# Four-layer kernel: layer 2's rows, projections and later norms prepared in another order

## The chip, the cores and the metric

The kernel runs on one core of a Trainium2 chip. The metric is the device time of one execution in microseconds. A profiled execution gives, besides its time, the work of each engine: TensorE (PE, with its weight loads shown apart as PEld), VectorE (DVE), ScalarE (ACT), GpSimd (POOL) and SyncE (SP), and the clock that TensorE was granted, as a share of full speed.

## The reference

Two sequences of 1024 tokens with 128 features pass four layers. Every layer has the same frame:

```python
xn = _layernorm(x, axis=-1)
s = attn(xn)                 # another kind of attention in each layer
g = _silu(ffn(xn))
x = x + s * g
```

The change is in layer 2. Its branch s is linear attention: a layer norm of xn (eps 1e-5, with weights), a projection to q, k, v, a gate, and running sums:

```python
x_norm = (x - mu) / jnp.sqrt(var + 1e-05) * ln_g + ln_b
q, k, v = jnp.split(x_norm @ w_qkv + b_qkv, 3, axis=-1)
gate_sig = jax.nn.sigmoid(x @ w_gate + b_gate)
gate_norm = gate_sig / (jnp.mean(gate_sig, axis=-1, keepdims=True) + 1e-05)
q, k = elu(q * gate_norm) + 1.0, elu(k * gate_norm) + 1.0
# causal: out = q . cumsum(k v) / (q . cumsum(k) + 1e-05), then w_proj
```

Its branch ffn is a small transformer block: causal softmax attention (16 heads of 8 features, 4 groups that share keys and values), then a mixture of 8 experts of which each token takes 2:

```python
def rms_norm(x, w): return x / jnp.sqrt(jnp.mean(x * x, -1, keepdims=True) + 1e-06) * w
# rope on even and odd features: [xe * cos - xo * sin, xe * sin + xo * cos]
h = x + attention(rms_norm(x, norm1_w), Wq, Wk, Wv, Wo)   # Q, K, V all from rope(x)
h = h + moe(rms_norm(h, norm2_w), router_w, router_b, W1, b1, W2, b2, W3, b3)
```

The input x of both branches is xn, which already is a layer norm. Its mean over the features is 0, and its mean square is var / (var + 1e-5), from the moments of the x before it.

## The kernel before

The 2048 tokens are 16 tiles of 128 tokens (rows), in 4 groups of 4 tiles, 512 tokens each; groups 0 and 1 are the first sequence, 2 and 3 the second. A matrix product needs its input with features as rows, so tiles are transposed on PE (four 128x128 transposes into one PSUM bank, `to_feature_major`, line 293), and copied to SBUF by ACT or DVE in turn (`copy`, lines 282 and 284). All products go through one helper (line 287), so PE's rows are told apart by their tiles.

**End of layer 1.** For each group the experts' rows are summed (`fetch`, line 398), passed through SiLU (989), multiplied (990) and added to x (991), in the order of groups 0, 2, 1, 3.

**Layer 2, preparation.** `normalise` (line 320) takes the moments of a group's x (statistics and their aggregation, lines 310 and 311; the root on ACT between a DVE addition and a DVE reciprocal, 299 to 301), makes xn on DVE (325), and transposes it into xT. Then `Attention.prepare` (1338), for each sequence and group: the sum of squares of xn on ACT (333), a root, xw = xn times the row's factor times the norm's weights on DVE (1352), the rotation as four products, a difference and a sum on POOL (1360 to 1365), the transposes of the rotated rows xr into xrT; and after both groups of a sequence the products with the weights: kT (pk), four qT (pq), and va (pv). kT and qT are kept as a rounded part and a remainder: `parts` casts on ACT (1335) and then runs one DVE operation (1336). PSUM has 8 buffers here.

**Softmax attention** (`softmax_attention`, 1510) first makes its constants on DVE (1518 to 1524): rounded identity, ones, two masks, and four cleared tiles mp. Then come four pre-steps (-4 to -1) and 72 steps, one for each pair of a query tile and a key tile not after it. To know each query row's largest score ahead of its exponentials, the scores are computed twice: once as pm, with queries as rows, for the maxima (`maxima`, 1397; DVE's reduction, 1424; the negated maxima split in mp, 1436 and 1437; turned on PE as pmt and copied to mT, 1444), and once as psc, with keys as rows (`weights`, 1448), on which ACT runs the exponential (1468), and whose results PE multiplies with va (pat, `values`). `close` (1480) divides, projects and adds xn: h. `take` (1534) decides how many pieces of maxima go into a step, from what is left and when it is due. The pieces pm, pmt and those of `close` share three PSUM buffers (sm2, tag pm); psc has two of two banks, pat has one.

PE's instructions stand in the order in which this code is written (`manual_schedule`, line 1012). The orders of the other engines are made by a scheduler of the framework, in the whole program.

**After it**: the norm of h, the router, and `Dispatch`, which makes the lists of rows for each expert (up to dfrom, line 1176), and the first part of linear attention. `linear_attention` (1222) is a generator, run forward a group at a time at the start, in the middle and at the end of the expert blocks. For each group it takes moments of xn, makes xl (1242), transposes it to xlT, multiplies with wq (128x384) and xT with the gate's weights, adds the biases (qg), and goes on to the gate (sig, gsum), qk (1263 to 1267), kv (1280) and the running sums. The expert blocks (1055 to 1078) load 256 rows each, and DVE, ACT and PE take part in all.

Of the kernel before, what the change touches and what calls it, by code (L numbers as in the profile page):

```python
# [19 lines left out]
P = 128  # L20
# [252 lines left out]
class Kern:  # L273
# [46 lines left out]
    def normalise(self, pool, ps, x, xn, xT, xs=None):  # L320
        for g in range(NG):
            mv, rs = self.moments(pool, lambda j: x[:, g * G + j, :], G, 1e-5, "ln")
            for j in range(G):
                i = g * G + j
                self.nc.vector.tensor_scalar(xn[:, i, :], x[:, i, :], mv[:, j, 0:1], rs[:, j : j + 1], ALU.subtract, ALU.mult)  # L325
            if xs is not None:
                keep_rows(self, xs, xn, g)
            self.to_feature_major(ps, lambda i: xn[:, i, :], xT, g)
# [665 lines left out]
def layer2(K, x, xn, xT, w, inp):  # L994
# [3 lines left out]
    with ExitStack() as es:  # L998
# [3 lines left out]
        with ExitStack() as e1:  # L1002
            pf = e1.enter_context(tc.tile_pool(name="f2", bufs=1))
            seqs = [Attention(K, pf, xn, w, h, b) for b in range(NB)]
            with tc.tile_pool(name="sn2", bufs=8, space=PSUM) as sn, tc.tile_pool(name="p2", bufs=1) as pp:
                K.normalise(pp, sn, x, xn, xT)
                for a in seqs:
                    a.prepare(pp, sn)
# [3 lines left out]
            with tc.manual_schedule(engines={mybir.EngineType.PE}):  # L1012
                with ExitStack() as e3:
# [3 lines left out]
                    softmax_attention(K, pf, sm, sc, so, seqs)  # L1017
        with ExitStack() as e2:
# [20 lines left out]
            linear = linear_attention(K, pa, sa, xn, xT, w, s)  # L1039
# [182 lines left out]
def linear_attention(K, pa, sa, xn, xT, w, s):  # L1222
# [7 lines left out]
    wq, bq = two("wq", [P, 384]), two("bq", [P, 512])  # L1230
# [4 lines left out]
    nc.vector.tensor_scalar_mul(wq, w["wqkv"], w["g"])  # L1235
    for g in range(NG):
        first = g % (NG // NB) == 0
        kvs = nc.vector if g < NG // NB else nc.gpsimd
        xl = two("xl", four)
        mv, rs = K.moments(pa, lambda j: xn[:, g * G + j, :], G, 1e-5, "la")  # L1240
        for j in range(G):
            nc.vector.tensor_scalar(xl[:, j, :], xn[:, g * G + j, :], mv[:, j, 0:1], rs[:, j : j + 1], ALU.subtract, ALU.mult)
        pt = sa.tile(four, F32, name="pxl", tag="ps")
        for j in range(G):
            nc.tensor.transpose(pt[:, j, :], xl[:, j, :], c["ident"])
        xlT = two("xlT", four)
        K.copy(xlT, pt)
        qg = two("qg", [P, G, 512], 2)
        sig, gsum = two("sig", four), two("gsum", [P, G])
        for j in range(G):  # L1250
            i = g * G + j
            pq = sa.tile([P, 512], F32, name="pqg", tag="ps")
            K.mm(pq[:, :384], xlT[:, j, :], wq)
            K.mm(pq[:, 384:], xT[:, i * P : (i + 1) * P], w["wg"])
            nc.vector.tensor_add(qg[:, j, :], pq, bq)
# [65 lines left out]
class Attention:  # L1321
# [16 lines left out]
    def prepare(self, pp, sc):  # L1338
        K, pf, xn, w, b = self.K, self.pf, self.xn, self.w, self.b
        nc, c = K.nc, K.c  # L1340
        four = [P, G, P]
        xrT = pp.tile([P, SEQ], F32, name="xrT", bufs=2)
        rs = pp.tile([P, TPB], F32, name="ars", bufs=2)
        for g in range(TPB // G):
            tiles = range(b * TPB + g * G, b * TPB + g * G + G)
            gr = rs[:, g * G : (g + 1) * G]
            for j, i in enumerate(tiles):
                K.sumsq(pp, gr[:, j : j + 1], xn[:, i, :])
            K.rsqrt(gr, gr, 1.0 / P, 1e-6)
            xw = pp.tile(four, F32, name="xw", bufs=2)  # L1350
            for j, i in enumerate(tiles):
                nc.vector.scalar_tensor_tensor(xw[:, j, :], xn[:, i, :], gr[:, j : j + 1], w["n1"], ALU.mult, ALU.mult)
            pair = xw.rearrange("p t (f two) -> p t f two", two=2)
            xe, xo = pair[:, :, :, 0], pair[:, :, :, 1]
            at = slice(g * G, g * G + G)
            cos, sin = w["cos"][:, at, :], w["sin"][:, at, :]
            xr = pp.tile(four, F32, name="xr", bufs=2)
            t2 = pp.tile([P, G, 64], F32, name="t2", bufs=2)
            t3 = pp.tile([P, G, 64], F32, name="t3", bufs=2)
            nc.gpsimd.tensor_mul(xr[:, :, :64], xe, cos)  # L1360
            nc.gpsimd.tensor_mul(t2, xo, sin)
            nc.gpsimd.tensor_sub(xr[:, :, :64], xr[:, :, :64], t2)
            nc.gpsimd.tensor_mul(xr[:, :, 64:], xe, sin)
            nc.gpsimd.tensor_mul(t3, xo, cos)
            nc.gpsimd.tensor_add(xr[:, :, 64:], xr[:, :, 64:], t3)
            K.to_feature_major(sc, lambda i: xr[:, i % G, :], xrT, g)
        self.qT = qT = pf.tile([P, 4, SEQ], F32R, name="qT", bufs=2)
        self.kT = kT = pf.tile([P, SEQ], F32R, name="kT", bufs=2)
# [3 lines left out]
        for g in range(TPB // G):  # L1372
            cols = slice(g * 512, (g + 1) * 512)
            pk = sc.tile([P, 512], F32, name="pk", tag="ps")
            K.mm(pk, w["wk"], xrT[:, cols])
            self.parts(pp, kT[:, cols], pk, w["klow"])
            for j in range(4):
                pq = sc.tile([P, 512], F32, name="pq", tag="ps")
                K.mm(pq, w["wq"][:, j, :], xrT[:, cols])
                self.parts(pp, qT[:, j, cols], pq, w["qlow"])  # L1380
            pv = sc.tile([P, G, 32], F32, name="pv", tag="ps")
            for j in range(G):
                i = g * G + j
# [96 lines left out]
    def close(self, sb, sm):  # L1480
# [26 lines left out]
        return first, second, third  # L1507


def softmax_attention(K, pf, sm, sc, so, seqs):  # L1510

# [317 lines left out]
```

## Time and profile before

| what | us |
|---|---|
| median of three runs | 1370.8 |
| the three runs | 1370.8, 1363.27, 1372.84 |
| profiled execution, its own time | 1371.2 |
| its span (first to last instruction) | 1369.3 |
| layer 2: x of layer 1 complete | at 479.9 |
| first product of group 0's keys (pk) | at 505.26 |
| first mask of the pre-steps (pm) | at 530.46 |
| first step (psc) | at 555.26 |
| last exponential's step over | about 838.7 |
| last h | at 843.8 |
| dfrom (rows of the experts known) | at 911.3 |

The clock granted over the profiled execution was 0.887 of full speed. Times "at" count from the start of the span. A row of the timeline shows the start, the duration, the engine, the line, the operation, and out<-in tiles with their shapes; several instructions of one kind in a run are one row with a count (x4), whose duration is that of all. In square brackets stands the idle time before it and what ended it.

### The profile page before, as it was taken

To read this page: it belongs to the slowest core of one execution; us is meant where nothing else is said; L and a number is where in the kernel's file an instruction comes from. 1 tells how busy PE (TensorE), PEld (TensorE's weight loads), DVE (VectorE), ACT (ScalarE), POOL (GpSimd) and SP (SyncE) were. 2 spreads that over 40 slices of the span, in tenths; PEclk is the share of its full clock that TensorE was granted. 3 is DMA by queue.
4 is the path that set the end of the run, shared out by engine and by line. 5 is a ranking of instruction groups with operands and counts; after the bars stand their busy time and mean duration, and the time that the engine had idled before them with its cause. 6 is when DMAs were issued, how large, how long until landed. Compare 5 with 4: busy or idle time off the path is not lost. (4 is left out here: it accounts for less than half of the span.)

```text
span 1369.3 us, 19321 instructions
## 1 busy us (share of the span) xinstructions
PE 1134.2 (83%) x6861; PEld 793.5 (58%) x6861; DVE 885.1 (65%) x2216; ACT 634.7 (46%) x1072; POOL 425.2 (31%) x420
## 2 busy tenths in 40 slices
PE   5599866888898748999999998679989918799985
PEld 2277455787798425544444433458778815577664
DVE  6536445875665686577787753988657469566456
ACT  7665926215413232344455576233452316355761
POOL 0352160027455150000000000034766521467743
PEclk9899885899999757699999998769999967799997
DMA  2000003014344200000000000024344530233411
GB/s 89 0 1 1 0 15 122 1 59 157 105 136 134 62 0 1 1 1 1 1 1 1 1 1 24 8 89 117 111 131 126 155 104 24 70 85 96 78 54 47
DMA packets 49040, 75.72 MB, mean 55 GB/s; under 512 B 7335, under 2 KB 36402, under 8 KB 48688
## 3 DMA queue, kind: packets, MB, share of 16 engines
q1 hardware_dynamic: 39632, 54.30, 12.7%
q0 software_dynamic: 8448, 14.98, 5.0%
q10 hardware_dynamic: 864, 5.21, 1.1%
q8 instruction: 54, 0.88, 0.3%
q14 instruction: 42, 0.34, 0.1%
HBM read 63.95 MB, written 12.85 MB: 56 GB/s over the span
## 5 line engine op out<-in xcount | busy, mean ns | idle before, releaser
L1424 DVE TENSOR_REDUCE mx<-pm 128x1 f32<-128x512 f32 (+3 forms) x304 | 182.1, 656 | 65.6 <-PE pm L287 62.6
L1468 ACT ACTIVATE pr<-psc 128x1024 f32<-128x1024 f32 x144 | 139.6, 1021 | 103.9 <-PE psc L287 68.2
L1188 POOL DMA_INDIRECT xb<-xs,dfrom x132 | 131.7, 998 | 123.2 <-PE pxb L797 31.5
L1198 POOL DMA_INDIRECT ys<-yb,dto x132 | 137.0, 1038 | 95.3 <-DVE yb L1076 44.4
L1163 POOL TENSOR_TENSOR dhh<-dhh,w_c 128x1280 fp32r<-128x1280 f32 (+2 forms) x3 | 8.8, 2927 | 480.3 <-issue 385.6
L287 PE MATMUL pm<-kT,qT 32*128 32x128 f32 (+3 forms) x576 | 119.3, 364 | 15.5 <-DVE mx L1424 11.4
L287 PEld LDWEIGHTS pm<-kT,qT 32*128 32x128 f32 x576 | 68.8, 203 | 68.3 <-DVE mx L1424 48.2
L287 PE MATMUL p<-xbT,tw 128*128 128x256 f32 x368 | 100.6, 391 | 1.7 <-ACT sg L1069 1.4
L1069 ACT ACTIVATE sg<-p,tw 128x256 f32<-128x256 f32 x92 | 40.8, 472 | 94.9 <-PE p L287 87.2
L287 PE MATMUL pat<-pr,va 128*32 128x512 f32 x576 | 81.0, 630 | 0.2 <-ACT pr L1468 0.2
L293 PE MATMUL tp<-w_c,xn 128*128 128x128 f32 x64 | 19.5, 412 | 67.7 <-DVE xn L325 40.3
L287 PEld LDWEIGHTS p<-xbT,tw 128*128 128x128 f32 x368 | 63.4, 194 | 12.3 <-ACT sg L1069 3.5
L287 PE MATMUL psc<-qT,kT 32*128 32x512 f32 x288 | 64.8, 487 | 3.0 <-ACT pr L1468 3.0
L1070 DVE SCALAR_TENSOR_TENSOR hh<-p,tw,sg 128x256 f32<-128x256 f32 x92 | 42.6, 479 | 35.6 <-ACT sg L1069 24.0
L287 PEld LDWEIGHTS po<-tw,hh 128*128 128x128 f32 x368 | 54.6, 193 | 5.8 <-DVE hh L1070 1.1
L287 PE MATMUL po<-tw,hh 128*128 128x128 f32 x368 | 56.7, 277 | 0.4 <-DVE hh L1070 0.4
L293 PEld LDWEIGHTS tp<-w_c,xn 128*128 128x128 f32 x64 | 11.5, 187 | 75.8 <-issue 38.7
L287 PE MATMUL psc<-mT,onesR 32*128 32x512 f32 x288 | 54.5, 410 | 0.0
L282 ACT COPY xbT<-pxb 128x256 f32<-128x256 f32 (+3 forms) x38 | 15.2, 401 | 61.0 <-PE pxb L797 44.9
L287 PEld LDWEIGHTS psc<-qT,kT 32*128 32x128 f32 x288 | 31.4, 188 | 15.9 <-ACT pr L1468 13.6
L287 PE MATMUL pcum<-kv,w_c 128*128 128x512 f32 x64 | 35.3, 652 | 2.1 <-DVE prod L1286 1.6
L287 PE MATMUL pd<-uda,w_c 128*128 128x512 f32 x64 | 34.9, 647 | 0.9 <-ACT usz L517 0.9
(531 smaller groups left out, 2840.6 us busy)
## 6 DMA issues: line engine op xcount, KB each, us to landing
tw<-in_rows SPq DMA_DIRECT2D x23, 836.0 KB, 4.8
tw<-in_rows SPq DMA_DIRECT2D x39, 384.0 KB, 3.2
yt<-ys SPq DMA_DIRECT2D x24, 256.0 KB, 3.0
tw<-in_rows SPq DMA_DIRECT2D x47, 128.0 KB, 2.2
xb<-xs,dfrom POOLq DMA_INDIRECT x132, 3.3
ys<-yb,dto POOLq DMA_INDIRECT x132, 2.3
xs<-xn SPq DMA_DIRECT2D x8, 256.0 KB, 2.3
w_l<-in_l ACTq DMA_DIRECT2D x1, 1890.0 KB, 11.1
```

Source lines behind the costliest of these rows:

```text
L282: self.nc.scalar.copy(out, in_)
L287: self.nc.tensor.matmul(out, lhsT=lhsT, rhs=rhs, start=start, stop=stop)
L293: self.nc.tensor.transpose(pt[:, j, :], src(g * G + j), self.c["ident"])
L1069: nc.scalar.activation(sg, p1[:, k - k0, :], AF.Silu, bias=t[:, 1536 + k : 1537 + k])
L1070: nc.vector.scalar_tensor_tensor(hh[:, k, :], p2[:, k - k0, :], t[:, 1540 + k : 1541 + k], sg, ALU.add, ALU.mult)
L1163: nc.gpsimd.tensor_mul(h, h.bitcast(F32), c["slot"][:, at].unsqueeze(2).to_broadcast(shape))
L1188: self.K.nc.gpsimd.indirect_dma_start(dst, None, self.xs, bass.IndirectOffsetOnAxis(self.of_token[:, n : n + 1], 0))
L1198: d = self.K.nc.gpsimd.indirect_dma_start(self.ys, bass.IndirectOffsetOnAxis(self.to[:, n : n + 1], 0), src, None, bounds_check=2 * T - 1, ...
L1424: nc.vector.tensor_reduce(mx[:, starts.index(a), g, j : j + k], tile[0][:, : k * m].rearrange("p (j m) -> p j m", m=m), AX.X, ALU.max)
L1468: K.nc.scalar.activation(pr, ps, AF.Exp, scale=scale)
```

## The change

The first sequence's first group (512 tokens) gets its rows and projections ahead of the softmax attention. The statistics of all groups are taken there too, and the rows of group 1. Group 1's projections, cut into seven parts (turn, keys, four queries, values), go into the pre-steps -3 to -1. Groups 2 and 3 get their rows at steps 4 and 13 as the code is written, and their parts at steps 7 to 13 and 16 to 22. The transposes of xn into xT go into steps 23 to 26. All of these take their PSUM from the three buffers of pm. A table `there` keeps maxima from being taken before their group is made.

The row factors: the mean square of xn comes from the moments (`mean_squares`), and its root serves the norm before the attention (ar, eps 1e-6), as a scale in a copy on ACT, and the linear attention's norm (r2, eps 1e-5), as a factor on the products of the untouched xT. The first norm's weights are multiplied into four tables of cosines and sines. The linear attention so loses its own statistics, norm, transposes and copy, and multiplies xT with one matrix 128x512. The attention's constants are made on POOL instead of DVE.

The diff, cut to its core (`rotate` keeps the other four operations on POOL as they were; `begin` makes qT, kT and va with its two memsets on POOL):

```diff
--- layer2
             seqs = [Attention(K, pf, xn, w, h, b) for b in range(NB)]
-            with tc.tile_pool(name="sn2", bufs=8, space=PSUM) as sn, tc.tile_pool(name="p2", bufs=1) as pp:
-                K.normalise(pp, sn, x, xn, xT)
-                for a in seqs:
-                    a.prepare(pp, sn)
+            ms = keep.tile([P, NT], F32, name="ms")
+            pp = e1.enter_context(tc.tile_pool(name="p2", bufs=1))
+            shared = attention_constants(K, pf, w)
+            n1 = w["n1"].rearrange("p (f two) -> p f two", two=2)
+            turn = {}
+            for n, a in (("cos", 0), ("sin", 0), ("cos", 1), ("sin", 1)):
+                turn[n, a] = pp.tile([P, TPB, 64], F32, name=f"{n}{a}")
+                nc.gpsimd.tensor_mul(turn[n, a], w[n], n1[:, :, a].unsqueeze(1).to_broadcast([P, TPB, 64]))
+            def measure(g):
+                at = slice(g * G, (g + 1) * G)
+                moments[g] = mv, rs = K.moments(pp, lambda j: x[:, g * G + j, :], G, 1e-5, f"ln{g}")
+                K.mean_squares(ms[:, at], mv, rs)
+                K.rsqrt(ar[:, at], ms[:, at], 1.0, 1e-6)
+            def rows(g):
+                mv, rs = moments[g]
+                for j in range(G):
+                    i = g * G + j
+                    nc.vector.tensor_scalar(xn[:, i, :], x[:, i, :], mv[:, j, 0:1], rs[:, j : j + 1], ALU.subtract, ALU.mult)
+                seqs[g // (NG // NB)].rotate(pp, g, ar, turn)
+            def columns(g, ps, tag):
+                pt = ps.tile(four, F32, name="tp", tag=tag)
+                for j in range(G):
+                    nc.tensor.transpose(pt[:, j, :], xn[:, g * G + j, :], c["ident"])
+                K.copy(xT[:, g * G * P : (g + 1) * G * P], flat(pt))
+            for a in seqs:
+                a.begin()
+            with tc.tile_pool(name="sn2", bufs=8, space=PSUM) as sn:
+                measure(0)
+                rows(0)
+                for part in seqs[0].projections(pp, 0, sn, "ps"):
+                    part()
+                for g in range(1, NG):
+                    measure(g)
+                rows(1)
...
-                    softmax_attention(K, pf, sm, sc, so, seqs)
+                    fill, there = [], {0: -4}
+                    parts = seqs[0].projections(pp, 1, sm, "pm")
+                    fill += [(-3 + n // 3, part) for n, part in enumerate(parts)]
+                    there[1] = -3 + (len(parts) - 1) // 3
+                    s0 = 4
+                    for g in range(2, NG):
+                        fill.append((s0, lambda g=g: rows(g)))
+                        parts = seqs[1].projections(pp, g, sm, "pm")
+                        fill += [(s0 + 3 + n, part) for n, part in enumerate(parts)]
+                        s0 = there[g] = s0 + 2 + len(parts)
+                    fill += [(s0 + 1 + g, lambda g=g: columns(g, sm, "pm")) for g in range(NG)]
+                    softmax_attention(K, pf, sm, sc, so, seqs, shared, fill, there)
--- linear_attention
-    wq, bq = two("wq", [P, 384]), two("bq", [P, 512])
+
+    wq, bq = two("wq", [P, 512]), two("bq", [P, 512])
+    r2 = two("r2", [P, NT])
+    K.rsqrt(r2, ms, 1.0, 1e-5)
     pb = sa.tile([P, 384], F32, name="pb", tag="ps")
     K.mm(pb, w["b"].to_broadcast([P, P]), w["wqkv"])
     nc.vector.tensor_add(bq[:, :384], pb, w["bqg"][:, :384])
     nc.scalar.copy(bq[:, 384:], w["bqg"][:, 384:])
-    nc.vector.tensor_scalar_mul(wq, w["wqkv"], w["g"])
+    nc.vector.tensor_scalar_mul(wq[:, :384], w["wqkv"], w["g"])
+    nc.scalar.copy(wq[:, 384:], w["wg"])
     for g in range(NG):
         first = g % (NG // NB) == 0
         kvs = nc.vector if g < NG // NB else nc.gpsimd
-        xl = two("xl", four)
-        mv, rs = K.moments(pa, lambda j: xn[:, g * G + j, :], G, 1e-5, "la")
-        for j in range(G):
-            nc.vector.tensor_scalar(xl[:, j, :], xn[:, g * G + j, :], mv[:, j, 0:1], rs[:, j : j + 1], ALU.subtract, ALU.mult)
-        pt = sa.tile(four, F32, name="pxl", tag="ps")
-        for j in range(G):
-            nc.tensor.transpose(pt[:, j, :], xl[:, j, :], c["ident"])
-        xlT = two("xlT", four)
-        K.copy(xlT, pt)
         qg = two("qg", [P, G, 512], 2)
         sig, gsum = two("sig", four), two("gsum", [P, G])
         for j in range(G):
             i = g * G + j
             pq = sa.tile([P, 512], F32, name="pqg", tag="ps")
-            K.mm(pq[:, :384], xlT[:, j, :], wq)
-            K.mm(pq[:, 384:], xT[:, i * P : (i + 1) * P], w["wg"])
-            nc.vector.tensor_add(qg[:, j, :], pq, bq)
+            K.mm(pq, xT[:, i * P : (i + 1) * P], wq)
+            nc.vector.tensor_add(qg[:, j, 384:], pq[:, 384:], bq[:, 384:])
+            nc.vector.scalar_tensor_tensor(qg[:, j, :384], pq[:, :384], r2[:, i : i + 1], bq[:, :384], ALU.mult, ALU.add)
--- Attention.rotate
+        xw = pp.tile(four, F32, name="xw", bufs=2)
+        for j in range(G):
+            i = g * G + j
+            nc.scalar.activation(xw[:, j, :], self.xn[:, i, :], AF.Copy, scale=ar[:, i : i + 1])
...
+        nc.gpsimd.tensor_mul(xr[:, :, :64], xe, cose)
+        nc.gpsimd.tensor_mul(t2, xo, sino)
--- Attention.projections
+        def turn():
+            pt = ps.tile([P, G, P], F32, name="tp", tag=tag)
             for j in range(G):
-                i = g * G + j
-                K.mm(pv[:, j, :], xrT[:, i * P : (i + 1) * P], w["wv"])
-            nc.vector.tensor_copy(va[:, g * G : (g + 1) * G, :, :8], pv.rearrange("p t (g d) -> p t g d", d=8))
+                nc.tensor.transpose(pt[:, j, :], self.turned[g][:, j, :], c["ident"])
+            made["xrT"] = pp.tile([P, G * P], F32, name="xrT", bufs=2)
+            K.copy(made["xrT"], pt.rearrange("p a b -> p (a b)"))
+        def keys():
+            pk = ps.tile([P, 512], F32, name="pk", tag=tag)
+            K.mm(pk, w["wk"], made["xrT"])
+            self.parts(pp, self.kT[:, cols], pk, w["klow"])
+        def queries(j):
+            pq = ps.tile([P, 512], F32, name="pq", tag=tag)
+            K.mm(pq, w["wq"][:, j, :], made["xrT"])
+            self.parts(pp, self.qT[:, j, cols], pq, w["qlow"])
+        def values():
+            pv = ps.tile([P, G, 32], F32, name="pv", tag=tag)
+            for j in range(G):
+                K.mm(pv[:, j, :], made["xrT"][:, j * P : (j + 1) * P], w["wv"])
+            nc.vector.tensor_copy(self.va[:, n * G : (n + 1) * G, :, :8], pv.rearrange("p t (g d) -> p t g d", d=8))
+        return [turn, keys, *(lambda j=j: queries(j) for j in range(4)), values]
--- attention_constants (from softmax_attention)
+    nc.gpsimd.tensor_copy(shared["ident"], c["ident"])
+    nc.gpsimd.tensor_copy(shared["ones"], c["ones"])
     for n in ("nge", "nle"):
-        nc.vector.tensor_copy(shared[n], seqs[0].w[n].unsqueeze(1).to_broadcast(four))
+        nc.gpsimd.tensor_copy(shared[n], w[n].unsqueeze(1).to_broadcast(four))
     shared["mp"] = [pf.tile(four, F32R, name=f"mp{n}") for n in range(4)]
     for t in shared["mp"]:
-        nc.vector.memset(t.bitcast(F32), 0.0)
+        nc.gpsimd.memset(t.bitcast(F32), 0.0)
+    return shared
--- softmax_attention
+        plan[-1]["from"] = there[n // G]
     later = {}
+    for s, part in fill:
+        later.setdefault(s, []).append(part)
...
+            if s < p["from"]:
+                break
```

## The prediction

> **What bounds the kernel now.** I read first the page's totals, to see which engine could be the limit, then the busy time by window over layer 2's first half, then the timeline of the same stretch, then the waits inside the softmax steps. The totals (engine, busy us, share of the span, instructions):
>
> ```profile
> PE 1134.2 (83%) x6861; PEld 793.5 (58%) x6861; DVE 885.1 (65%) x2216; ACT 634.7 (46%) x1072; POOL 425.2 (31%) x420
> ```
>
> No engine is full over the whole span, so each stage needs its own reading. In the windows the columns are the window, its us, the busy us and instructions of PE, PEld, DVE, ACT, POOL, then the granted clock:
>
> ```profile
> 482.00:490.00 8.00, 2.40 (x8) 1.46 (x8) 7.72 (x39) 4.09 (x22) 0.00 (x0) 0.50 0.00 0
> 490.00:500.00 10.00, 4.47 (x12) 2.20 (x12) 9.82 (x29) 4.44 (x21) 7.76 (x11) 0.50 0.00 0
> 510.00:520.00 10.00, 9.76 (x42) 5.70 (x41) 7.36 (x12) 5.27 (x9) 0.16 (x1) 1.00 0.00 0
> 540.00:550.00 10.00, 8.36 (x36) 5.67 (x35) 6.18 (x10) 0.59 (x1) 0.00 (x0) 0.50 0.00 0
> 600.00:620.00 20.00, 19.04 (x149) 9.96 (x145) 15.89 (x32) 8.70 (x11) 0.00 (x0) 1.00 0.00 1
> 860.00:900.00 40.00, 24.95 (x89) 15.54 (x89) 38.59 (x114) 8.69 (x13) 2.98 (x1) 0.73 0.15 56
> ```
>
> The reader is to see four regimes. From 482 to 500 DVE is full (norms) and PE nearly idle at half clock. From 510 to 530 PE is full at clock 1.00 (projections). In the pre-steps (540 to 550) the clock is back at 0.50. In the steps (600 to 620) PE is 95% busy and DVE 79%. After the steps DVE is 96% busy. Four rows of the timeline (start, us, engine, line) mark the borders, and two more give a price:
>
> ```profile
> 479.21 0.68 DVE L991 TENSOR_TENSOR x<-x,acc 128x512 f32<-128x512 f32 x1
> 486.78 1.11 DVE L325 TENSOR_SCALAR xn<-x,lnmv,lnrs 128x128 f32<-128x128 f32 x4
> 490.96 2.94 DVE L325 TENSOR_SCALAR xn<-x,lnmv,lnrs 128x128 f32<-128x128 f32 x4
> 505.26 1.91 PE L287 MATMUL pk<-xrT,w_l 128*128 128x512 f32 x2
> 530.46 0.70 PE L287 MATMUL pm<-ngeR,identR 128*128 128x512 f32 x2 [0.94 <-DVE va L1385]
> 555.26 1.91 PE L287 MATMUL psc<-nleR,identR 128*128 128x512 f32 x4
> ```
>
> So the preparation is 479.9 to 530.46 (50.5 us), the four pre-steps 530.46 to 555.26 (24.8), the 72 steps 555.26 to 838.7 (3.94 us each). The waits from 560 to 840 (who waited, for whom: total us, times, longest) agree with a nearly full PE, for ACT and DVE both wait for it:
>
> ```profile
> ACT pr L1468 <- PE psc L287: 68.2, 48, 3.8
> PEld pm L287 <- DVE mx L1424: 51.8, 105, 0.9
> DVE mx L1424 <- PE pm L287: 50.6, 54, 4.9
> ```
>
> The second row is the three-buffer ring of mask scores: PE loads the next weights only when DVE's reduction has freed a buffer.
>
> **Part 1: the preparation.** It loses the projections of groups 1 to 3, which ran on PE from 512.47 to 529.5 (17.1 us). Group 0's own run, from 505.26 to 512.47 (7.2 us), stays, with 1 us to the first mask (pv's copy, then pm, as at 529.5 to 530.46). The start of group 0 moves too, because it no longer waits for both groups of its sequence (the second transposes, 504.35). Gone from DVE are casts and memsets of constants (1.00 + 0.48 + 0.51 + 0.41 + 2.11 = 4.5 us) and 16 xw products (7.3 us, 3.1 of them beside POOL); gone from ACT are 16 squares with their reads (0.48 each, 7.7 us), as the mean square now comes from the moments; 16 row scalings come to ACT at 0.385 each (line 1665's row, the same operation), 6.2 us. The 16 transposes of xn leave PE's queue here, where they stood ahead of group 0's rotated rows (498.85).
>
> Against this stands POOL. It now makes four turn tables (the 128x512 products of lines 970 and 1697 took 1.10 to 1.19: 4.6 us), casts four constants (128x512 copies on POOL took 0.61: 2 at that and 2 of a quarter of the size, 1.5), fills four mp (va's memsets, 1.84 for 2048 columns, give 0.46 each: 1.8) and va (2.2 with its ones), in this order, all ahead of group 0's rotation. From the last read of layer 1 that they wait for, 477.1, that is 10.1 us: 487.2. Then POOL's order has group 0's four products (3.0), group 1's four (3.0), and only then group 0's difference and sum (1.5): 494.7 at the earliest, and 497 if group 1's xn is as slow as the row at 490.96. Transposes (1.1) and copy (0.6) make 497 to 499; ACT's copy stands in its queue behind row scalings of groups 2 and 3, which wait for POOL's products to free their two buffers, 3 us more. I take 502 for group 0's first projection, bounds 498 and 506. With 7.2 and 1.0 the first mask is at 510.2, against 530.46: **-20** (-24 to -15).
>
> DVE's xn took 1.11 us for four beside an idle POOL and 2.94 beside POOL's products. The Trainium skill's "SBUF — State Buffer", section "Who interferes with whom", calls this an exclusive lock between DVE and GpSimd, which a tensor_scalar can meet, and so speaks against constants on POOL; the trace agrees as far as these two rows go. By that rule all four groups' xn would fall into POOL's work, 4 x 1.8 = 7 us longer instead of the 3.5 seen in two of them, and the first projection would be at about 505.
>
> That rows 512 and on are prepared "amid the steps" holds for their projections. In DVE's and ACT's orders all 16 xn and all 16 scalings stand in the preparation, so their cost is in the 502 already, and steps 4 and 13 get none.
>
> **Part 2: group 1 in the pre-steps.** Seven parts. On PE at the clock seen there (0.50): a key or query pair 1.91, five times, 9.6; four transposes 1.1; pv 1.9 (twice its 0.97): 12.6 us. PE was idle 20% of these 24.8 us, and DVE, at 62%, takes its 5 x 0.75 in gaps; 3.6 of the 12.6 go into the idle time: **+9**. Bounds: +6 (the pace of full clock, 5.2 to 6.1) and +12.6 (nothing hidden). Cover gone, all of it shows, because the chain from masks to mT sets the first step.
>
> **Part 3: 18 fills in the steps.** Groups 2 and 3 give seven parts each in steps 7 to 13 and 16 to 22, xT's four column groups one each in steps 23 to 26. At clock 1.00 a query pair is 0.90 (513.41: 3.60 for four), pv 0.97, four transposes about 0.6: 2 x (4.5 + 0.97 + 0.6) + 4 x 0.6 = 14.5 us of PE. PE is 95% busy, so nearly all of it is time; **+15**. Below: the 4 us of idle PE in those 20 steps take some and the clock (0.50 at 580 to 588) is lifted by denser work, +9. Above: a fill takes a buffer of the ring, and PE stops until it has passed: 0.90, 0.25 to ACT, 0.58, 0.75 on DVE, less the 1.0 us in which other buffers go on, 1.5 each for ten and about 1 for eight, +23. Behind a waiting pm load on PE stand the step's score matmuls, and ACT's exponentials wait for these.
>
> **Part 4: linear attention.** Up to dfrom (911.3) DVE loses 16 statistics (0.2), 16 aggregations (0.1), four root chains (0.32) and 12 norms (0.34): 10.2 us. Eight adds of 128x512 at 0.68 become 128x128 at 0.29 and 128x384 at 0.56: +1.4. The order then puts one more qk (1.23) and two more kv (1.22) ahead of dfrom, +3.7, and ACT's queue has six table loads (1.28) between the last head and the first exponential where it had four, +2.6. That leaves 10.2 - 1.4 - 3.7 - 2.6 = 2.5 gained if every wait falls well in a stretch where DVE is 96% full; as PE and ACT feed it, I take **-1** (-7, which is without the loads and half of what was pulled ahead, to +3). In the expert blocks PE is nearly full (5.7 us a block), and the last two groups lose 8 transposes (0.41) and 8 short matmuls with their weight loads (about 0.1 of exposed time): **-4** (-5 to 0).
>
> **Sum.** -20 + 9 + 15 - 1 - 4 = -1. The profiled execution took 1371.2 us (span 1369.3, 1.9 around it); the median of the runs is 1370.8, so both scales agree. Forecast **1370**.
>
> **Rivals.**
> (a) *Hidden fills.* DVE has 21% free and ACT over half; if the parts slip into PE's issue gaps and the clock stays up from 510 on, the low ends hold: -22 + 6 + 9 - 4 - 5 = -16, up to -20: about 1355. For: 24.8 us of pre-steps and much of 564 to 588 run at 0.50, which denser work could lift. Against: PE is 95% busy in the steps.
> (b) *The ring becomes the bound*, the slower side. Place: steps 7 to 26. A projection holds one of three mask buffers for 0.9 + 0.25 + 0.6 + 0.2 + 0.75 = 2.7 us (PE, ACT, DVE), and when DVE's queue is in a run of five reductions (3.08 us at one place) longer. If PE stands for 2.3 us at each of 18 fills, that is 41 instead of 15: 1396. It decides from 1.65 us a fill (30 in all, +14 with the other terms). For: 105 waits of PE's loads on the reductions already. Against: none of them is over 0.9 us.
> (c) *It doesn't do what it says*: POOL's 10 us of tables, and the rows of all groups kept in the preparation, eat the gain of group 0: first mask at 518 instead of 510, sum +7: 1378.
>
> **Chances.** About 1% (13.7 us) is what a measurement here can tell from no change. Forecast 0.37 and (c) 0.12, both inside; (a) 0.25; (b) 0.26. Range: from (a)'s far end, 1351, to short of (b)'s full price, 1393; the open bounds of parts 1 to 3 make the same width.
>
> **What would show it.** Right: first mask near 510, clock 0.50 in the pre-steps, steps 7 to 26 longer by 0.8 us each and PE over 95% busy in them, last h near 848 (843.8 before), dfrom near 914, expert blocks 4 us shorter. The Trainium skill's "TensorE: Matmul & The Clock Gate", section "What's actually happening", has the clock rise after about 3.4 us of busy PE; here it rose 3 to 5 us after 505.26 and fell again at 534, so by that page a denser pre-step would run at 1.00 and part 2 would be +6. Wrong: waits of PE's loads on kT, qT or mx of over 1 us in the steps (then b), a first projection after 508 (then c), or pre-steps at clock 1.00 (then a).

## The result, and the profile after

The changed kernel takes 1387.46 us (median of six runs, 1384.9 to 1390.01) against 1370.87 before (six runs): a ratio of 1.0127, 95% interval 1.0101 to 1.0153. It is slower by 16.6 us, where 0.8 us faster was forecast. The profiled execution took 1386.34 us, its span is 1384.6, 15.3 more than before.

The totals of the page, in the same columns as the line shown of before:

```profile
PE 1156.9 (84%) x6813; PEld 806.7 (58%) x6813; DVE 868.8 (63%) x2160; ACT 631.2 (46%) x1052; POOL 431.7 (31%) x432
```

DVE has 16 us less to do, as the change meant. PE has 48 instructions fewer and is busy 22.7 us longer, so its instructions became slower on average: this is the first sign of the clock. The timeline of the changed kernel at the borders of its stages (start, us, engine, line):

```profile
482.34 0.66 DVE L994 TENSOR_TENSOR x<-x,acc 128x512 f32<-128x512 f32 x1
486.23 3.79 DVE L1030 TENSOR_SCALAR xn<-x,ln0mv,ln0rs 128x128 f32<-128x128 f32 x4
490.21 1.11 DVE L1030 TENSOR_SCALAR xn<-x,ln1mv,ln1rs 128x128 f32<-128x128 f32 x4
503.23 2.07 PE L287 MATMUL pk<-xrT,w_l 128*128 128x512 f32 x2 [0.68 <-ACT xrT L282]
511.11 0.70 PE L287 MATMUL pm<-ngeR,identR 128*128 128x512 f32 x2 [0.94 <-DVE va L1446]
545.38 1.91 PE L287 MATMUL psc<-nleR,identR 128*128 128x512 f32 x4
```

The reader sees the first mask at 511.1 instead of 530.5 and the first step at 545.4 instead of 555.3: the steps start 9.9 us earlier. Windows of the changed kernel (window, us, busy us of PE, PEld, DVE, ACT, POOL, granted clock):

```profile
483.00:494.00 11.00, 0.00 (x0) 0.00 (x0) 10.47 (x49) 3.35 (x11) 6.37 (x11) 0.50 0.00 0
511.00:545.00 34.00, 26.72 (x108) 16.17 (x109) 19.91 (x36) 3.85 (x7) 2.79 (x4) 0.68 0.00 1
618.00:632.00 14.00, 13.90 (x56) 7.55 (x55) 6.05 (x11) 4.67 (x6) 0.00 (x0) 0.54 0.01 2
632.00:668.00 36.00, 33.67 (x225) 16.75 (x225) 26.91 (x48) 17.74 (x22) 0.00 (x0) 0.99 0.00 0
670.00:681.00 11.00, 11.00 (x52) 6.13 (x51) 5.36 (x11) 2.99 (x4) 0.00 (x0) 0.53 0.01 1
```

Two stretches amid the steps ran at half clock: 13.7 us from 619.1 on and 10.2 us from 670.3 on. Before, the stretch from step 6 to step 26 (the start of ACT's exponentials of these steps) ran almost wholly at full clock:

```profile
594.01:678.91 84.90, 80.39 (x578) 38.70 (x577) 66.92 (x132) 42.78 (x50) 0.00 (x0) 0.98 0.00 1
```

Waits from 560 to 855 hardly differ from those of before, and so do not show where the time went:

```profile
ACT pr L1531 <- PE psc L287: 70.2, 52, 3.8
DVE mx L1487 <- PE pm L287: 47.5, 51, 4.9
PEld pm L287 <- DVE mx L1487: 45.4, 97, 0.8
```

The stages, each as the time since the one above it; "step 6" is the start of that step's exponential on ACT:

| up to | before | after | difference |
|---|---|---|---|
| x of layer 1 complete | 479.9 | 483.0 | +3.1 |
| first mask (pm) | 50.6 | 28.1 | -22.5 |
| first step (psc) | 24.8 | 34.3 | +9.5 |
| step 6 | 38.8 | 38.8 | 0 |
| step 26 | 84.9 | 110.4 | +25.5 |
| last h | 164.9 | 164.9 | 0 |
| dfrom | 67.3 | 71.0 | +3.7 |
| x of layer 2 | 210.4 | 204.3 | -6.1 |
| end | 247.7 | 249.8 | +2.1 |

The later runs were on other chips, on which the kernel before takes about 1421 us; the layers before, the expert blocks and the last layer last longer there. From x of layer 1 to the last h it took 363.9 us in the first trace and 368.2 and 362.4 in two later ones, which goes with the clock (see the table below). So totals are compared as ratios to the kernel before on the same chip, and stages of layer 2 directly; where an expectation names a total in us, it is on the scale of the first chip (1370.87 for the kernel before). The two later traces of the kernel before are of executions 0.6% and 1.0% slower than its median there, so only stages are read from them.

### The profile page after: what moved, and what is told of

It is laid out like the page before. It is cut to its first block, busy times and chain, and to the rows that moved or that the text cites. A ratio compares the mean times of both kernels' runs of the same rounds, so it can differ in the third digit from the quotient of the medians.

```text
span 1384.6 us, 19131 instructions
## 1 busy us (share of the span) xinstructions
PE 1156.9 (84%) x6813; PEld 806.7 (58%) x6813; DVE 868.8 (63%) x2160; ACT 631.2 (46%) x1052; POOL 431.7 (31%) x432
## 5 line engine op out<-in xcount | busy, mean ns | idle before, releaser
L287 PE MATMUL pm<-kT,qT 32*128 32x128 f32 (+3 forms) x576 | 122.1, 364 | 17.0 <-DVE mx L1487 11.2
L287 PEld LDWEIGHTS p<-xbT,tw 128*128 128x128 f32 x368 | 63.7, 194 | 15.2 <-issue 4.3
L287 PE MATMUL psc<-qT,kT 32*128 32x512 f32 x288 | 65.7, 495 | 3.0 <-ACT pr L1531 3.0
L293 PE MATMUL tp<-w_c,xn 128*128 128x128 f32 x48 | 14.2, 419 | 47.5 <-DVE xn L1730 27.0
```

Of the source, the lines that this page charges most:

```text
L287: self.nc.tensor.matmul(out, lhsT=lhsT, rhs=rhs, start=start, stop=stop)
L293: self.nc.tensor.transpose(pt[:, j, :], src(g * G + j), self.c["ident"])
```

## The experiments

**The price of a fill, taken apart.** Three theories were left for the 25.5 us: PE's own work, the mask buffers that a fill holds, and DVE's queue. Two kernels keep the fills and leave out parts of them. In the first, keys and queries of groups 2 and 3 are not converted (the queries' line is shown, the keys' is alike, and POOL writes zeros in their place):

```diff
+            if g < 2:
+                self.parts(pp, self.qT[:, j, cols], pq, w["qlow"])
```

> Groups 2 and 3 keep their transposes, products with the weights and values in steps 7 to 22, but no engine reads the products for keys and queries: their kT and qT are zeros written on POOL ahead of the pre-steps, so this kernel leaves out the second sequence's real keys and queries. From the trace of the changed kernel, steps 6 to 26 cost 25.5 us (exponentials 9.9 us earlier than before at step 6, 15.6 later at step 26). Theory R (a fill holds one of the three mask buffers until ACT and DVE are done): PE's own work is 14.5 of it, so about 10 us go: 1377 against 1387. Theory P (PE's own work is all of it, buffers are free in time): at most 2 us go: 1385 or more.

Steps 6 to 26 took 95.7 us; the ratio to before was 1.0032 (0.9997 to 1.0068), 1375 us on the first chip's scale. In the second, ACT writes the rounded value and DVE's multiply-add is left out:

```diff
+            self.parts(pp, self.qT[:, j, cols], pq, w["qlow"]) if g < 2 else nc.scalar.copy(self.qT[:, j, cols], pq)
```

> In groups 2 and 3 ACT writes kT and qT directly as rounded values and DVE's multiply-add is left out, so the remainders of those keys and queries are missing from the result. It keeps PE's and ACT's share of a fill and takes DVE's 0.75 us out of ten of them. Theory R: the buffer comes free after ACT, about 1 us earlier in ten fills, some of it hidden: 1380 to 1383. If DVE's queue is the cause (the multiply-add stands ahead of reductions that PE waits for): all of what the first run gains, about 1377. Theory P: 1386 or more.

97.0 us, ratio 1.0053 (1.0022 to 1.0084), or 1378 us. So ACT's ten casts cost 1.3 us and DVE's ten multiply-adds 13.4, 1.34 each for an instruction of 0.75. That PE's own work is all of the loss falls with this. Buffer or queue is told apart by a kernel that ends the buffer's use early, and one that takes DVE out:

```diff
+        self.K.nc.scalar.copy(raw, src)          # the buffer is free
+        self.K.nc.scalar.copy(high, raw)
+        self.K.nc.vector.scalar_tensor_tensor(dst, high.bitcast(F32), low, raw, ALU.mult, ALU.add)
```

> Groups 2 and 3: ACT copies a product to SBUF first, which ends the use of the mask buffer; ACT then rounds from SBUF and DVE's multiply-add (0.75 us, same place in DVE's queue) reads SBUF. The stretch from the exponential of step 6 to that of step 26 took 84.9 us before, 110.3 with the change, 95.8 with PE's part alone and 96.9 without the multiply-add. Theory slot (the buffer held until the multiply-add has read it): 97 to 100, since the buffer is freed 0.6 us after the product. Theory queue (the multiply-add itself stands in DVE's queue ahead of reductions that PE waits for): 107 to 112, the second rounding on ACT included.

107.3 us, ratio 1.0152 (1.0089 to 1.0215): the time for which the buffer is held is not what costs. With POOL's three instructions after the first copy:

```diff
+        self.K.nc.gpsimd.tensor_copy(high, raw)
+        self.K.nc.gpsimd.tensor_scalar(part, high.bitcast(F32), low, None, ALU.mult)
+        self.K.nc.gpsimd.tensor_add(dst, part, raw)
```

> As the run before, but rounding, multiplication and addition are done by POOL (three instructions), so DVE has nothing of the keys' and queries' conversion. Both theories: 96 to 99 for steps 6 to 26 (as without the multiply-add). Should it stay above 105, neither the slot nor DVE's queue is the cause but the conversion's end (kT and qT late for the maxima).

100.4 us, above the 96 to 99 expected, ratio 1.0018 (0.9989 to 1.0046). Both readings so far would name DVE's queue. The stretch from step 6 to step 26 as one window, first of the changed kernel, then of the one without the multiply-add, then with the products alone, shows another thing:

```profile
584.14:694.52 110.38, 104.18 (x638) 53.40 (x637) 76.69 (x147) 49.98 (x62) 0.00 (x0) 0.89 0.00 1
```

```profile
589.95:686.93 96.98, 92.52 (x638) 46.33 (x637) 69.59 (x137) 50.02 (x62) 0.00 (x0) 1.00 0.00 1
```

```profile
596.17:691.89 95.72, 91.73 (x638) 46.04 (x637) 69.53 (x137) 44.55 (x53) 0.00 (x0) 1.00 0.00 1
```

PE runs the same 638 instructions in all three; its clock is 0.89 in the first and 1.00 in the others. The first spent 23.9 us at half clock. If the same products take half of that at full clock, the stretch would be 98.4: by this estimate the multiply-adds as such are worth 1.4 us, and the halved clock 12.0.

**The clock.** In the changed kernel PE waited for a multiply-add just ahead of the first fall (timeline):

```profile
614.18 1.13 PE L287 MATMUL pq<-xrT,w_l 128*128 128x512 f32 x2
615.97 0.75 DVE L1384 SCALAR_TENSOR_TENSOR qT<-high,w_l,pq 128x512 fp32r<-128x512 f32 x1
616.77 0.49 PE L287 MATMUL pm<-kT,qT 32*128 32x512 f32 x2 [0.54 <-DVE qT L1384]
619.06 1.93 PE L287 MATMUL pat<-pr,va 128*32 128x512 f32 x8
```

The last row takes 1.93 us; the same row six us earlier (613.19) took 1.06. Two kernels tested this: one gives PE other work ahead of the wait, the other adds products that are overwritten.

```diff
+        if s in filled:      # steps with a key or query fill
+            next(w, None)    # step scores first
+            rows(before)
```

> In the ten steps that hold a key or query fill, PE's step scores (psc) are put ahead of the masked rows' scores, so that PE has work that needs no mask buffer while DVE finishes the fill's multiply-add. Clock theory: with the change PE stood 0.54 us for a multiply-add at 616.2, the granted clock fell to 0.50 for 13.4 us from 619 and again for 10.4 us from 670, and this half-speed time (24 us, a loss of 12) is what the multiply-add costs; without the wait the clock stays at 1.00 and steps 6 to 26 take 97 to 100 us instead of 110.3. Queue theory (the multiply-add's 0.75 us and its wait are lost once per fill, whatever the clock): 107 to 111 with the clock at 1.00 all along.

113.1 us at a clock of 0.89, ratio 1.0167 (1.0109 to 1.0224). The falls came at other places, again 23.9 us in all: the order did not take PE's waits away (it now stood 0.67 us for a reduction at 626.6), so this settles nothing.

```diff
+        else:
+            for g in range(more):   # 2 in fill steps
+                K.mm(bank(g), shared["ident"], shared["nle"], True, True)
```

> The changed kernel with two additional products of 128x512 (0.27 us each at full clock) in each fill step that has no masked tile, written into the step's own score banks before the mask scores and then overwritten: about 5 us more work for PE, nothing less. Clock theory: if the added work fills PE's wait enough to keep the clock, steps 6 to 26 take 99 to 104 us, less than the 110.3 without it; if it does not, both drops stay and it is about 113. Queue theory: 113 to 116 and no connection with the clock.

The window of step 6 to step 26 of this kernel:

```profile
598.56:701.85 103.29, 98.44 (x654) 50.17 (x653) 76.69 (x147) 50.00 (x62) 0.00 (x0) 0.98 0.00 1
```

Sixteen products more, DVE's and ACT's work unchanged to 0.02 us, and 7.1 us less time. A theory in which every fill costs its own wait does not give that. The ratio was 1.0087 (1.0055 to 1.0119). Are the falls chance? The changed kernel and the one before were traced again.

> The changed kernel once more. If the two falls of the clock in steps 6 to 26 (619 to 632 and 670 to 681 in the first trace, 35 and 86 us after the exponential of step 6) belong to the change, they come again at about the same places, with 20 us or more at 0.50 and 107 to 111 us for the stretch. If they are chance, the stretch takes 98 to 103.

> The kernel before once more. Its first trace had 3.4 us at half clock in steps 6 to 26 (84.9 us), a later one on another chip 19.4 us (89.0). If the first is typical: 84 to 86. If falls of the clock are as frequent before as with the change: 88 or more.

> The kernel before, for its stages on the chip of these runs: steps and preparation as in its first trace (75.4 us from x to the first step, 84.9 for steps 6 to 26, 67.3 to dfrom); expert blocks, layers 0, 1 and 3 longer than there, as their transfers are slower on this chip. If x of layer 1 comes more than 3 us earlier than in the runs above, or the last layer is over 3 us shorter, then the change costs something outside layer 2 too.

The changed kernel gave 110.38 us at 0.89 once more, with 23.9 us at half clock at the same places (ratio 1.0116, 1.0042 to 1.0191); the kernel with the old linear attention below, whose steps are the same, gave 110.4 and 23.9 too. The kernel before gave 89.0 us in one run, with 13.7 us at half clock (the 19.4 us of the expectation take in some that lie ahead of step 6), and 83.5 with none; its own ratios to itself were 1.0025 (0.9970 to 1.0080) and 0.9984 (0.9945 to 1.0022). So before, the falls come and go; with the change they stood in three traces of three. All of it in one table, steps 6 to 26; the last column takes off half of the time at half clock, as above, and is an estimate. The last two kernels, described below, have no projections in these steps, and fell all the same:

| kernel | us | clock | of it at half clock | at full clock |
|---|---|---|---|---|
| before, three traces | 84.9, 89.0, 83.5 | 0.98, 0.92, 1.00 | 3.4, 13.7, 0 | 83.2, 82.2, 83.5 |
| all ahead, only xT's columns in the steps | 85.7 | 1.00 | 0 | 85.7 |
| fills, products alone | 95.7 | 1.00 | 0 | 95.7 |
| with ACT's casts | 97.0 | 1.00 | 0 | 97.0 |
| the change, three traces | 110.4 | 0.89 | 23.9 | 98.4 |
| buffer freed early | 107.3 | 0.94 | 13.7 | 100.5 |
| conversion on POOL | 100.4 | 0.97 | 6.8 | 97.0 |
| step scores first | 113.1 | 0.89 | 23.9 | 101.2 |
| 16 products added | 103.3 | 0.98 | 3.4 | 101.6 |
| groups 1 to 3 in the pre-steps | 89.4 | 0.94 | 10.2 | 84.3 |
| all ahead, products added in early steps | 88.5 | 0.96 | 6.8 | 85.1 |

What goes ahead of a fall can be read from all 18 traces, before, after and experiments. The changes of the clock lie on a grid of windows of 3.41 us. By their shapes the products of kT and qT (into pm and psc) and of mT have 32 rows, the masks and all others here 128. For each window, from 60 us ahead of the first exponential to the last one, take the time in which PE ran a product, count a product on 32 rows as a quarter of its time, and divide by 3.41. At full clock, each of the 61 windows with a share under 0.36 was followed by half clock, 24 of the 85 from 0.36 to 0.45, and 9 of the 1349 with more. At half clock, full clock came back after 1 of 152 windows under 0.70 and after 109 of 182 with more. In the changed kernel the windows ahead of the two falls have 0.26 and 0.32, though PE was busy for 0.81 and 0.89 of them; without the multiply-adds no window of steps 6 to 26 is under 0.42, and with the sixteen products none is under 0.44 (its one fall followed a window of 0.54). So it is not a wait alone that goes with a fall, but a wait in a window that is filled with products on few rows. This is a reading of traces; no run changed the rows alone.

**All projections ahead.**

```diff
+                for g in range(1, NG):
+                    rows(g)
+                    for part in seqs[g // (NG // NB)].projections(pp, g, sn, "ps"):
+                        part()
```

> All four groups are projected ahead of the pre-steps with eight PSUM buffers, as in the kernel before; row factors, constants on POOL, transposes of xn in steps 23 to 26 and the new linear attention stay. If the loss is the interleaving: first mask near 528 (510 plus 17 of projections), first step near 553, steps longer by 2.5 us for the transposes alone, the same 3.8 us loss up to dfrom and 6.0 us gain in the expert blocks: about 1369. If the loss comes from elsewhere in the change: above 1380.

From x to the first step 73.4 us (75.4 before, 62.4 with the change), steps 6 to 26 85.7, x to the last h 359.6, against 363.9, 368.2 and 362.4 in the three traces of before and 376.5 with the change. Up to the last h the expectation about held. The total did not follow: the ratio, 1.0073 (1.0039 to 1.0107), is 1381 us on the first chip's scale, where 1369 was expected and above 1380 if the loss comes from elsewhere. Part of it is dfrom (+3.7) and the expert blocks, which gained 6.1 us on the first chip and nothing on these: 215.9 us here and 215.9 in the change's second trace, against 214.7 and 213.9 for the kernel before. The rest is not explained.

**Groups 1 to 3 in the pre-steps**, in the PSUM banks of the step scores, which are empty until step 0:

```diff
+                    banks = Pairs(sc)
+                    parts = seqs[0].projections(pp, 1, banks, "ps")
+                    for g in range(2, NG):
+                        parts += seqs[1].projections(pp, g, banks, "ps")
```

> All 21 parts of groups 1 to 3 go between the mask scores of the four pre-steps, and use the four PSUM banks of the step scores, which are empty until step 0, instead of the mask ring. If the in-step fills are the loss, steps 6 to 26 are back at 85.7 (as with all projections ahead). The pre-steps then last 34 us if PE, now dense, gets the full clock, or 24.8 + 3 x 9 = 52 at half clock; I expect 40. With 28 us from x to the first mask that is 68 from x to the first step, against 75 before and 62 with the change: total 0.995 to 1.003 of before. Rival: the conversions stand ahead of reductions in DVE's queue there too, and the pre-steps take 52 or more: 1.005.

The pre-steps took 58.3 us, as the rival has it. Ratio 1.0145 (1.0095 to 1.0195). The place is another than the rival's: in the waits of that stretch PE's loads wait 11.2 us and its products 8.3 us for DVE's multiply-adds ahead of products into the score banks (psc), that is for a bank to be read out, and only 1.9 us ahead of masks (pm) for reductions. The mean clock there is 0.65. Steps 6 to 26 took 89.4 us and not 85.7, with 10.2 us at half clock. The same kernel with one dependence more:

```diff
+    nc.vector.tensor_scalar(zero, after[:, NT - 1 :], 0.0, None, ALU.mult)
+    nc.vector.tensor_scalar(bq[:, 384:], w["bqg"][:, 384:], zero, None, ALU.add)
```

> The run before, and the gate's bias is made to depend on the fourth root of the row norms of h, so that the first group's sigmoids cannot stand between roots in ACT's queue: four table loads of 1.28 us instead of six up to the first exponential. If the loads make the loss between last h and dfrom (67.3 before, 71.0 with the change), this stretch falls to 67 to 68. If the work of the second group that stands ahead of dfrom makes it, it stays at 70 to 71.

Last h to dfrom fell from 71.0 to 68.2 us, with three table loads up to and with the first exponential's instead of seven, so 2.8 of the 3.7 go with the loads. The other kernels agree: 67.4 to 68.8 us in the three below with this dependence, 70.3 to 71.1 in all others with the new linear attention. In the changed kernel ACT goes back and forth between the tables of roots and sigmoids, and DVE, in the last row, waits for it:

```profile
865.56 1.28 ACT L1304 ACT_TABLE_LOAD   x1
867.86 1.28 ACT L300 ACT_TABLE_LOAD   x1
869.15 0.20 ACT L300 ACTIVATE rs<-rs 128x4 f32<-128x4 f32 x1
869.38 1.28 ACT L1304 ACT_TABLE_LOAD   x1
869.39 0.18 DVE L301 RECIPROCAL rs<-rs 128x4 f32<-128x4 f32 x1 [1.35 <-ACT rs L300]
```

The total's ratio, 1.0108 (1.0022 to 1.0194), is too wide to show 2.8 us.

**The linear attention of before in the changed kernel.**

```diff
-            linear = linear_attention(K, pa, sa, xT, ms, w, s)
+            linear = linear_attention(K, pa, sa, xn, xT, w, s)
```

> The changed kernel with the linear attention of before (own statistics, norm, transposes, two products). If the new linear attention causes both the 3.8 us loss between the last h and dfrom and the 6.0 us gain in the expert blocks, the two go back to 67.5 and 188 us and the total is 1390. If the loss up to dfrom has another cause (fewer free engines, placement), that stretch stays at 71 and the total is 1393.

65.7 us to dfrom instead of 71.0, and 220.2 in the expert blocks instead of 215.9 (the change's second trace, also on a chip with slow transfers): the new one loses 5.3 us ahead of dfrom and gains 4.3 after it, each from one trace. Ratio 1.0179 (1.0136 to 1.0222), 1395 us on the first chip's scale; by the two stages it should be 1 us below the change, whose ratios were 1.0127 and 1.0116. The intervals overlap, and no run tells more.

**Towards a better version.** All projections ahead, sigmoids after the roots, and the constants on ACT instead of POOL (one of them is shown):

```diff
-        nc.gpsimd.memset(t.bitcast(F32), 0.0)
+        nc.scalar.activation(t, w["nge"].unsqueeze(1).to_broadcast(four), AF.Copy, scale=0.0)
```

> All projections ahead, the gate's bias after the fourth root, and the attention's constants made by ACT, which idled 5.6 us before the first root. From the traces: x to first step 73 or less (75.4 before), steps 6 to 26 85.7 (84.9), last h to dfrom 68.2 (67.3), expert blocks 5 to 6 us shorter, x of layer 1 up to 2 us later: 0.993 to 0.998 of before, if nothing outside layer 2 moves. With the same measured excess that the other run with all projections ahead had over its stages (about 9 us), 1.000 to 1.005.

x to the first step 73.2 us, to the last h 359.2, h to dfrom 68.8; ratio 1.0024 (0.9991 to 1.0057): no difference to the kernel before, and better than the change. Two further ones add overwritten products there.

```diff
+            for g in range(2):       # after each batch of mask tiles in the pre-steps
+                K.mm(spare[:, g], shared["ident"], shared["nle"], True, True)
```

> All projections ahead, constants on ACT, the gate's bias after the roots, and two additional products of 128x512 after each batch of three mask tiles in the pre-steps, into the step scores' empty banks. Clock theory: PE's waits for the reductions are filled, the clock stays at 1.00 after the projections, and the pre-steps take 17 to 21 us instead of 25.0. Work theory (the added products cost their time, about 0.5 us a batch): 27 to 31.

> The run before with two such products also in the steps 0 to 7 that have no mask of their own (five of the eight). Clock theory: the steps from the first exponential to that of step 6, 32.5 us at a clock of about 0.7, take 27 to 31. Work theory: 34 to 36.

The clock theory's expectation failed for the pre-steps. From the first mask to the first exponential it took 34.0 us, against 27.9 without the products, 6.1 more, where the work theory has 2 to 6; ratio 1.0043 (1.0015 to 1.0070). The window of the first of these kernels:

```profile
540.00:566.00 26.00, 26.00 (x85) 16.58 (x85) 13.90 (x27) 0.84 (x2) 0.00 (x0) 0.50 0.00 0
```

PE was busy for 26.00 of 26.00 us, and the clock stayed at 0.50. Weighted by rows as above, the windows of this stretch have shares of 0.52 to 0.88. In the early steps the added products did what was expected, 30.7 us instead of 33.1 up to step 6, but steps 6 to 26 were 2.8 us longer, with 6.8 us at half clock, ratio 1.0058 (1.0020 to 1.0096). No version was found that beats the kernel before.

## Why the prediction was wrong

**Part 1, right, in part by luck.** -20 was forecast for the first mask and -19.4 measured (530.5 to 511.1), with the first projection at 503.2 for a forecast of 502. POOL's order came as read, but two terms missed and cancelled: POOL stood 4.95 us for the roots of the row factors and ended group 0's rotation at 501.4, not at 494.7 to 497; and ACT's copy did not stand 3 us behind row scalings, it started at 502.59 when the transposes were done. The longer xn came: four xn took 3.79 us beside POOL's fills and 1.11 after them. The Trainium skill's "SBUF — State Buffer", section "Who interferes with whom", describes an exclusive lock between DVE and GpSimd that a tensor_scalar can meet, here against memsets, which only write; the two rows agree. x of layer 1 came 3.1 us later, 0.9 of it in one of its products (line 993), which took 1.56 instead of 0.66 beside POOL's tables; this is inside the -19.4.

**Part 2, right in size, not in its terms.** +9 forecast, +9.5 measured. The forecast was 12.6 us of PE at clock 0.50, of which 3.6 hide in idle time. Measured, PE was busy 27.1 us instead of 19.5, so 7.6 more, at a mean clock of 0.68 (0.56 before), and its idle time did not shrink but grew, from 5.3 to 7.2. The two errors cancelled, which is luck. The first exponential came 1.3 us sooner after that, as its table was loaded earlier, and the next steps gave this back.

**Part 3, wrong: this is the step that failed.** "At clock 1.00 a query pair is 0.90", and so +15, at most +23. Measured: +25.5. The PE work was sized right: at full clock the stretch would be 98.4, against 83.2 before: +15.2. The runs divide it, from the 83.5 of the trace without falls: xT's columns 2.2 (to 85.7), products, values and turns 10.0, casts 1.3, multiply-adds about 1.4, together 14.9. The other 10.3 us are the clock: half of 23.9 us, less half of the 3.4 us that the first trace of before had. What failed is the clock of 1.00 that the term took for granted. Its lower bound let denser work lift the clock; its upper bound counted buffers and queues at full clock. That a fill could halve the clock for 24 us was on neither side, although the trace of before had one such fall in the steps, 3.4 us at half clock near 622.

**Rival (b)** had the side and the place, steps 7 to 26, and a total of 1396 for 1387; its mechanism fell, since freeing the buffer early took only 3.1 of the 25.5 us away, and these 3.1 are less time at half clock (at full clock the stretch grew, from 98.4 to 100.5). At 1.42 us a fill it also stayed below its own point of 1.65; the total passed 1% only together with part 4. (a) fell with the clock, (c) with the first mask at 511.

**Part 4, wrong in the first half.** -1 was forecast up to dfrom, +3.7 measured. DVE's busy time there fell by only 3.7 us (62.7 to 59.0), and the stretch became 3.7 longer, so its idle time grew from 4.6 to 12.0. The prediction named the loads (+2.6) and set DVE's savings against them. But in the trace of before the statistics and norms that were saved stand between the roots (844 to 851), where DVE waited for 0.7 us at most; now it stands 2.3 us for the first root (r), 1.35 and 1.30 for roots behind table loads, and 2.8 for PE's transposes of h's rows. The expert blocks gained 6.1 for a forecast of 4, on that chip only. The last layer, in which nothing was changed, took 2.1 us more; no run tells why.

The sum of the steps, with the measured terms: 3.1 - 22.5 + 9.5 + 25.5 + 3.7 - 6.1 + 2.1 = 15.3 us.

**What stays open.** That the clock's fall, and not the waits as such, makes about 10 of the 25.5 us is shown by the granted clock and by the kernel that did more work in 7 us less. That the multiply-adds bring the falls on rests on two kernels without them, one trace each. They are not the only thing that does: kernels with no projections in these steps had 0 to 13.7 us at half clock. The share of rows in use separates most windows ahead of a fall from the others, as the traces show it; why the clock stays at half above 0.70 in some windows and not in others is open: PE fully busy at 0.50 for 26 us does not fit the idea that waits alone do it.

## What to carry to other kernels

Matrix work that moves to a stage in which PE is nearly full costs its time there again; here 22.5 us of an earlier first mask bought 35 us later. Price such a move with the clock of the place it goes to, and look in the profile whether that clock falls there already: here the clock added 10.3 us to 15.2 us of work. In such a stage a short wait can cost far more than its own length (ten multiply-adds: 1.4 us by the estimate at full clock, 13.4 as measured). Where work is taken off an engine, ask first whether it is the one that is waited for: DVE's saved time ahead of dfrom was spent waiting for ACT's roots and the rows behind them.

## What the runs showed of the hardware

- The same 638 PE instructions took 97.0 us at a clock of 1.00 and 110.4 at 0.89 (the first without ten multiply-adds on DVE); half clock lasted 13.7 us after the first fall and 10.2 after the second, with PE busy throughout. In all 18 traces the clock is 1.00 or 0.50, and a stretch of either, apart from the first and last of a trace, lasts a multiple of 3.41 us.
- By the profile, in which the ends of products are modelled, PE was busy for 26 us on end at a clock of 0.50. The Trainium skill's "TensorE: Matmul & The Clock Gate", section "What's actually happening", has full clock after about 3.4 us of sustained activity. Taken as busy time of PE, this trace does not agree, and the measurement decides; the products there are a mix of some on 128 rows and some on 32.
- On other chips the kernel before took 1421 us instead of 1371. Its preparation with the pre-steps (75.4, 75.4 and 75.6 us in three traces) and the stretch from the last h to dfrom (67.3, 66.8 and 66.8) were the same to 0.5 us; the last layer took 286 us and more instead of 247.7.
